# A transformer block in float32 on one core: the copies of the values and the context's keys change their places in the self-attention's slots

## Chip, core and metric

The kernel runs on one core of a Trainium2 chip. The metric is the time of one execution on the device in microseconds (us). TensorE (PE) does matrix products, VectorE (DVE) row maxima and 32x32 transposes, ScalarE (ACT) exponentials and copies out of PSUM, GpSimd (POOL) elementwise work in SBUF, and SyncE (SP) issues nearly all DMAs, in the order in which its queue holds them.

## The reference

Two sequences `x` of 1024 rows by 256, and two contexts of 154 rows by 192, all in float32:

```
h = layernorm(x, ln1);  x = attention(h, h, sa_wq, sa_wk, sa_wv, sa_wo, sa_bo) + x
h = layernorm(x, ln2);  x = attention(h, context, ca_wq, ca_wk, ca_wv, ca_wo, ca_bo) + x
h = layernorm(x, ln3);  a, gate = split(h @ ff_w1 + ff_b1)
x = (a * gelu(gate)) @ ff_w2 + ff_b2 + x
```

Attention has 16 heads of 64 columns, with an ordinary softmax over the keys.

## The kernel before

**Units and slots.** A unit is one sequence and one pair of heads: 2 x 8 = 16 units, 0 to 15. The self-attention of a unit takes eight slots, so there are 128 slots p, with unit p // 8 and place n = p % 8 in it (SH = 4 is half a unit). The order on every engine is written out by hand: the main loop over p (line 1364 on) records one slot after the other, and each engine works off its own list. A slot is counted here on PE, from the first score product (L568) of p to the first of p + 1.

A slot p does this. PE computes the scores of 64 query rows, in two halves (`scores`, L568, two PSUM tiles; a tile is used again in the next slot, once its exponentials are taken). DVE takes their negated maxima (L577), ACT the exponentials and their sums (L585). Each row's keys lie in two halves on two groups of partitions, so the halves' maxima and sums must be exchanged: `exchange` (L595) issues four small DMAs on SP into the tile `st`, once both exponentials are there. In the next slot POOL takes the difference of the maxima (`differences`, L603 and L604, "dd"), ACT its exponential (L610, "ee"), POOL the denominator (L612, L614), and a slot later DVE its reciprocal (L683, "rd"), POOL weighs the exponentials with it (L691), and DVE transposes them (L718).

**Beside the scores** PE has one piece of other work in every slot: in n = 3, 4, 7 and 0 the product of the weights with the values (`self_values`, L624, "po"), in the other four what the list `work` holds: the queries (L395) and keys (L395) of the next unit, values (L427) of the next pair of units, or, in one slot per unit from unit 2 on, a round of the output projection (`out_rounds`, L532, "pr"). In a round the second half waits for a small copy `seen` (L541) on ACT, which stands between the exponentials of the same slot. A layer norm of other rows has its transposes (L307) in n = 5 of some units.

**Values.** `value_pieces` projects the values of units u and u + 1 in two pieces; the second is done in n = 2 of the even unit u, and ACT copies it to SBUF at the start of n = 3 (`store` in `project_self_values`, L437). The product needs each value also on the other 64 partitions: `half_moves` gives two DMAs a unit (L449, L450; 256 KB each). Those of unit u are issued at once in `store`, so on SP ahead of the exchange of n = 3; those of u + 1 go on the list `moves`, of which `load_ahead` issues one in n = 4 and one in n = 5, behind the exchange of that slot. The values of a unit are first read in its n = 7.

**Unit 0 is apart.** Its own queries, its values and those of unit 1 are projected in its slots 0 to 2 (values: two banks `mm_tile`), the queries and keys of unit 1 in slots 3 and 4. Beside them, from the list `side`, come turning the contexts (slot 0), the context's keys of pair 0 (slot 1), of pairs 1 and 2 (slot 2; `context_keys`, L881, 2 products a pair), and turning the rows of gains and shifts (`turn_rows`, L218, slot 3). Slot 5 has the keys of pairs 3 and 4, slot 6 those of pair 5. `context_ends` (L913), the last rows of the context's values for all pairs, is in slot 10, with a `sum_tile`, its weights `ca_wv_ends` (two DMAs of 384 KB, `load_ends`, L898) being issued in slot 4. The key weights of pairs 3 to 5 (`load_keys(3, 3)`, L123, 288 KB) replace those of pairs 0 to 2 in one buffer and are issued in slot 3.

**Weights.** `load_ahead(p)` runs behind the exchange of slot p. In units other than 0 it loads the query weights (L142) of unit u + 2 in n = 2 and its key weights (L142) in n = 6; in unit 0 these are n = 5 and 6. There is one buffer for key weights; they are used in n = 2 or 5 of unit u + 1. `later` holds writes of `ends` to DRAM (L922), popped in n = 2, 4 and 6; `to_dram` lists six slots in which keys go to DRAM (L844).

## Time and profile before

| | us |
|---|---|
| median of 3 runs | 1072.24 |
| the runs | 1070.6, 1072.24, 1075.17 |
| the profiled execution | 1069.05 |
| its span, first to last instruction | 1067.3 |
| scores of slot 0 begin | 17.62 |
| slot 17 (n = 1 of unit 2) begins | 111.25 |
| slot 120 (n = 0 of unit 15) begins | 654.89 |

In the rows of a timeline the first number is the start in us from the span's start, the second the length, then engine, line, operation, what is written and read, and the count of instructions merged into the row. A bracket at the end is idle time of that engine just before the row, and what ended it. Rows of SPq are issues of DMAs: their length is the issue, not the transfer.

### The profile page before, as it was taken

What the parts mean: (1) busy time and instruction counts of PE and PEld (TensorE: products, weight loads), DVE (VectorE), ACT (ScalarE), POOL (GpSimd) and SP (SyncE); (2) the same over time, 40 slices, a digit from 0 to 9 for tenths busy, and PEclk for the clock granted to TensorE, in tenths of its full rate; (3) what the DMA queues carried; (4) which work ended last, traced back from release to release, by engine and by line L of the source; (5) the groups of instructions that cost most, each with busy time, mean ns of one, the idle gap of its engine ahead of it and who ended that gap; (6) DMA issues with size and microseconds to landing.
All of it is one profiled execution on the core that took longest, in us unless ns stands there. A gap on an engine that the chain in (4) does not pass through costs nothing.

```text
span 1067.3 us, 51311 instructions
## 1 busy us (share of the span) xinstructions
PE 1051.0 (98%) x21700; PEld 731.4 (69%) x21700; DVE 882.2 (83%) x1321; ACT 658.6 (62%) x2147; POOL 767.1 (72%) x1604
## 2 busy tenths in 40 slices
PE   8999999999999999999999999999999999999998
PEld 6435755566566668775556686666777667789998
DVE  5689899999989999999999989978776777775654
ACT  5666667667776766766777767666556655243221
POOL 2577677778777787777777777768666677598783
PEclk9999999999999999999999999999999999999999
DMA  4231221121021121121111112135422221000000
GB/s 106 73 83 50 70 63 41 32 47 44 14 64 35 25 54 44 30 50 44 30 41 47 34 35 63 36 77 134 124 59 83 68 59 41 1 7 15 21 11 30
DMA packets 96887, 52.87 MB, mean 50 GB/s; under 512 B 30410, under 2 KB 95442, under 8 KB 96658
## 3 DMA queue, kind: packets, MB, share of 16 engines
q1 hardware_dynamic: 95330, 48.93, 18.6%
q8 instruction: 171, 2.80, 1.1%
q10 hardware_dynamic: 1328, 0.66, 0.2%
q14 instruction: 58, 0.48, 0.1%
HBM read 36.23 MB, written 4.39 MB: 38 GB/s over the span
## 4 chain that ended last, share of the span: by engine, by line
PE 84%; DVE 5%; POOL 3%; ACT 2%; SPq 2%; DMA 2%; issue 2%; DVEq 0%; POOLq 0%; ACTq 0%
PE po L624 18%; PE s L568 18%; PE py_ca L508 5%; PE pv_sa L427 5%; PE pf L1267 4%; PE pq_sa L395 4%; PE pr L532 4%; PE pk_sa L395 4%; PE poc L1042 4%; PE pb L1147 4%; PE pq_ca L395 4%; PE sc L977 3%; PE pa L1147 2%; PE pc L1147 2%; SPq L595 2%
## 5 line engine op out<-in xcount | busy, mean ns | idle before, releaser
L691 POOL TENSOR_SCALAR p<-p,rd,ee 128x512 f32<-128x512 f32 x508 | 385.1, 768 | 78.5 <-DVE rd L683 74.8
L585 ACT ACTIVATE p<-s,st 128x512 f32<-128x512 f32 x512 | 345.3, 685 | 142.7 <-DVE st L577 118.2
L577 DVE TENSOR_REDUCE st<-s 128x2 f32<-128x1024 f32 x256 | 308.5, 1206 | 52.8 <-PE s L568 16.5
L718 DVE STREAM_TRANSPOSE pT<-p 128x1024 f32<-128x1024 f32 x256 | 303.9, 1220 | 2.8 <-POOL p L691 2.8
L568 PE MATMUL s<-k_sa,q_sa 64*32 64x512 f32 x4096 | 256.9, 590 | 3.0 <-ACT p L585 2.4
L624 PE MATMUL po<-pT,v_sa 64*32 64x256 f32 x6144 | 181.0, 376 | 1.9 <-ACT p L995 1.5
L624 PEld LDWEIGHTS po<-pT,v_sa 64*32 64x32 f32 x6144 | 137.3, 106 | 51.4 <-issue 15.0
L568 PEld LDWEIGHTS s<-k_sa,q_sa 64*32 64x32 f32 x4096 | 99.2, 106 | 83.3 <-issue 46.3
L995 ACT ACTIVATE p<-sc,neg 128x154 f32<-128x154 f32 x256 | 96.9, 405 | 72.4 <-DVE rden L1003 70.4
L1006 POOL TENSOR_SCALAR p<-p,rden 128x154 f32<-128x154 f32 x256 | 96.8, 398 | 52.9 <-DVE rden L1003 51.9
L585 ACT ACTIVATION_READ_ACCUMULATOR p<-s,st 128x1 f32 x512 | 103.2, 201 | 0.0
L982 DVE TENSOR_REDUCE neg<-sc 128x6 f32<-128x924 f32 (+1 forms) x48 | 48.1, 1003 | 20.2 <-PE sc L977 20.0
L610 ACT ACTIVATE ee<-dd 128x8 f32<-128x8 f32 x128 | 26.7, 209 | 57.1 <-POOL dd L604 56.1
L508 PE MATMUL py_ca<-ca_wo,o_ca 128*128 128x256 f32 x256 | 61.1, 385 | 0.0
L624 PE MATMUL po<-pT,third_v 64*32 64x256 f32 x2048 | 60.2, 376 | 0.5 <-issue 0.5
L427 PE MATMUL pv_sa<-sa_wv,home 64*32 64x256 f32 x2048 | 59.4, 376 | 0.0
L624 PEld LDWEIGHTS po<-pT,third_v 64*32 64x32 f32 x2048 | 50.5, 106 | 12.8 <-issue 6.1
L395 PE MATMUL pq_ca<-home,ca_wq 64*128 64x512 f32 (+1 forms) x352 | 57.8, 589 | 0.0
L395 PE MATMUL pq_sa<-home,sa_wq 64*32 64x512 f32 (+1 forms) x976 | 57.8, 586 | 0.0
L427 PEld LDWEIGHTS pv_sa<-sa_wv,home 64*32 64x32 f32 x2048 | 46.4, 106 | 15.7 <-issue 5.4
L995 ACT ACTIVATION_READ_ACCUMULATOR p<-sc,neg 128x1 f32 x256 | 56.5, 221 | 0.0
L612 POOL TENSOR_TENSOR zz<-ee,st 128x8 f32<-128x8 f32 x128 | 25.9, 202 | 42.6 <-ACT ee L610 42.6
(142 smaller groups left out, 1604.1 us busy)
## 6 DMA issues: line engine op xcount, KB each, us to landing
st<-st SPq DMA_DIRECT2D x510, 1.0 KB, 2.1
v_sa<-v_sa SPq DMA_DIRECT2D x24, 256.0 KB, 3.8
v_ca<-vd SPq DMA_DIRECT2D x32, 160.0 KB, 3.5
sa_wq<-in_L_xattn_sa_wq_dram SPq DMA_DIRECT2D x32, 128.0 KB, 3.1
sa_wk<-in_L_xattn_sa_wk_dram SPq DMA_DIRECT2D x32, 128.0 KB, 3.2
sa_wv<-in_L_xattn_sa_wv_dram SPq DMA_DIRECT2D x32, 128.0 KB, 3.1
ca_wq<-in_L_xattn_ca_wq_dram SPq DMA_DIRECT2D x32, 128.0 KB, 4.6
wf<-in_L_xattn_ff_w_dram SPq DMA_DIRECT2D x12, 256.0 KB
```

The costliest lines, as they stand in the source:

```text
L395: nc.tensor.matmul(pq[r][f:f + m, at:at + n], lhsT=wt[own, c, f:f + m], rhs=h[own, c, t0:t0 + n], start=(c == 0), stop=(c == NH - 1), tile ...
L427: nc.tensor.matmul(pv[r][f:f + KB, i * VC:(i + 1) * VC], lhsT=h[own, c, t0:t0 + KB], rhs=wt[own, c, :], start=(c == 0), stop=(c == NH - 1) ...
L508: nc.tensor.matmul(py[:, e * D:(e + 1) * D], lhsT=o[:, i, (t + e) * P:(t + e + 1) * P], rhs=wo[kind, b, g][:, i, :], start=(i == 0), stop= ...
L568: nc.tensor.matmul(sc[a4 * KB:(a4 + 1) * KB, j, :], lhsT=q[r, c:c + KB], rhs=k[r, h * HB:(h + 1) * HB], start=True, stop=True, tile_positi ...
L577: nc.vector.tensor_reduce(st[:, 0, 0, i, :], sc, AX.X, ALU.max, negate=True)
L585: nc.scalar.activation(pr[:, j, :], sc[:, j, :], AF.Exp, bias=st[:, 0, 0, i, j:j + 1], accum_out=st[:, 0, 1, i, j:j + 1],)
L624: nc.tensor.matmul(po[a2][d:d + KB, :QH // 2], lhsT=v[r, t, e, d:d + KB], rhs=pT[r, d // DH * NK + n, :], start=(t == 0 and e == 0), stop= ...
L691: nc.gpsimd.tensor_scalar(pr[:, j, :], pr[:, j, :], v["rd"][:, c:c + 1], v["ee"][:, 0, c:c + 1], op0=ALU.mult, op1=ALU.mult,)
L718: nc.vector.transpose(halves[h][:, :, c:c + KB], slot[p]["members"][i].rearrange("p j (n k) -> p (j n) k", k=KB))
L995: nc.scalar.activation(pr_[:, j, i, :T], sc[:, j, i * T:(i + 1) * T], AF.Exp, bias=neg[:, j, i:i + 1], accum_out=den[:, j, i:i + 1],)
L1006: nc.gpsimd.tensor_scalar(pr_[:, j, i, :T], pr_[:, j, i, :T], rden[:, j, i:i + 1], 1.0, op0=ALU.mult, op1=ALU.mult,)
L1147: nc.tensor.matmul(into[:, :BT], lhsT=lhs, rhs=wh[pair][i], start=first, stop=True, skip_group_check=True)
```

## The change

All of it concerns the self-attention.

1. `store` of the values issues no move itself; all four go on `moves`, and `load_ahead` issues one in each of n = 3, 4, 5 and 6 of an even unit, behind that slot's exchange.
2. The context's keys of pairs 0 to 2 leave slots 1 and 2. The keys are now done three at a time (`three_keys`): pairs 0 to 2 in slot 5, pairs 3 to 5 in slot 10. `load_keys(3, 3)` follows the first three, in slot 5. `turn_rows` so comes in slot 1.
3. `context_ends` goes from slot 10 to slot 6, with an `mm_tile`. `load_ends` stays in slot 4. The writes of `ends` so begin four slots earlier.
4. The second value piece of unit 0 takes `sum_tile` banks.
5. The key weights are loaded in n = 7 instead of n = 6, in every unit. The query weights stay.

```diff
@@ store() of project_self_values
             if i0 + 2 == GT:
-                for move in half_moves(v[0]):
-                    move()
-                moves.extend(half_moves(v[1]))
+                for own in v:
+                    moves.extend(half_moves(own))
@@ value_pieces
-    def value_pieces(u, bank):
+    def value_pieces(u, banks):
...
-                [bank(f"pv_sa{u}_{i0}_{r}") for r in range(2)], wsl["sa", pr, "v"], hT["sa", b], i0)
+                [banks[i0 // n](f"pv_sa{u}_{i0}_{r}") for r in range(2)], wsl["sa", pr, "v"], hT["sa", b], i0)
@@ self_beside
             if ui == 1:
-                nxt.insert(1, costing(2, context_ends))
+                nxt.insert(1, costing(2, lambda: three_keys(3)))
             if ui % 2:
-                ahead_values.extend(value_pieces(ui + 1, sum_tile))
+                ahead_values.extend(value_pieces(ui + 1, (sum_tile, sum_tile)))
@@ load_ahead
-            if n != (2 if what == "q" and ui else 2 * SH - 2 - (what == "q")):
+            if n != (2 * SH - 1 if what == "k" else 2 if ui else SH + 1):
...
-        if moves and ui % 2 == 0 and n in (SH, SH + 1):
+        if moves and ui % 2 == 0 and n in range(SH - 1, 2 * SH - 1):
             moves.pop(0)()
...
-        if p == 3:
-            load_keys(3, 3)
@@ new
+    def three_keys(first):
+        return together(*(
+            lambda pr=pr, bank=bank: context_keys(pr, bank)
+            for pr, bank in enumerate((sum_tile, sum_tile, mm_tile), first)))
@@ context_ends
-        pe = sum_tile("pe")
+        pe = mm_tile("pe")
@@ before the main loop
-        side.append((True, (), lambda: context_keys(0, sum_tile)))
-        side.append((True, (), lambda: together(*(
-            lambda pr=pr: context_keys(pr, sum_tile) for pr in (1, 2)))))
         side.append((True, (), turn_rows))
...
-        work.extend(value_pieces(0, mm_tile))
+        work.extend(value_pieces(0, (mm_tile, sum_tile)))
@@ main loop over p
                 if p == SH + 1:
-                    for pr in (3, 4):
-                        run(lambda: context_keys(pr, mm_tile))
+                    run(lambda: three_keys(0))
+                    load_keys(3, 3)
                 elif p == SH + 2:
-                    run(lambda: context_keys(5, mm_tile))
+                    run(context_ends)
```

## The prediction

> **What bounds the kernel now.** First the page's span and a table of busy time by stage (after the span: length, PE busy, PEld, DVE, ACT, POOL, then PE's granted clock, DMA share, GB/s).

> ```profile
> span 1067.3 us, 51311 instructions
> 0.00:150.00 150.00, 141.29 (x3180) 87.41 (x3188) 118.64 (x158) 95.49 (x281) 91.91 (x198) 1.00 0.30 76
> 150.00:700.00 550.00, 548.82 (x14976) 357.81 (x14968) 513.28 (x611) 385.05 (x1166) 417.20 (x864) 1.00 0.17 41
> 700.00:1067.30 367.30, 360.88 (x3568) 286.19 (x3552) 250.26 (x554) 178.06 (x701) 257.99 (x544) 1.00 0.20 52
> ```

> PE is the bound. From 150 to 700 us it is idle 1.2 us of 550, in the first 150 us 8.7 us; nothing after 700 us is touched by the change. DVE is next, 513 of 550. A busy PE need not be at its best pace, so I read the timeline of PE: the time from the first score product of a slot to that of the next.

> ```profile
> 84.32 1.93 PE L568 MATMUL s<-k_sa,q_sa 64*32 64x512 f32 x32
> ...
> 89.49 1.93 PE L568 MATMUL s<-k_sa,q_sa 64*32 64x512 f32 x32
> ```

> That is 5.17 us, the pace of nearly every slot after slot 11: about 1.75 for scores, 3.45 beside them. The work on PE is the same before and after, so a gain can only be stretched slots made short. I find three places.

> **1. Unit 0 and what is moved in it** (slots 0 to 11). PE again; slots 2, 3 and 10 begin with the L568 rows at 28.72, 36.41 and 74.66, slot 12 with that at 84.32 above; the row at 65.18 is the second half of slot 8's scores.

> ```profile
> 28.72 1.95 PE L568 MATMUL s<-k_sa,q_sa 64*32 64x512 f32 x32
> ...
> 34.05 2.42 PE L881 MATMUL pk<-ctxT,ca_wk 96*128 96x320 f32 x8
> 36.41 1.95 PE L568 MATMUL s<-k_sa,q_sa 64*32 64x512 f32 x32
> ...
> 41.72 0.24 PE L218 MATMUL p_rows<-ident,rows 28*128 28x28 f32 x1
> ...
> 51.00 2.39 PE L881 MATMUL pk<-ctxT,ca_wk 96*128 96x320 f32 x8 [1.78 <-DMA ca_wk<-in_L_xattn_ca_wk_dram]
> ...
> 65.18 1.09 PE L568 MATMUL s<-k_sa,q_sa 64*32 64x512 f32 x16 [0.61 <-ACT p L585]
> ...
> 74.66 1.93 PE L568 MATMUL s<-k_sa,q_sa 64*32 64x512 f32 x32
> 76.52 1.92 PE L913 MATMUL pe<-ca_wv_ends,ctxT 96*32 96x512 f32 x16
> ```

> Slot 2 is 7.69 long, because two pairs of keys (2.42, so 1.2 a pair) follow the value piece. Slot 1 loses one pair (1.2) and gains the rows (0.24), slot 2 loses 2.42, slot 3 the rows. The sum is 3.6 us, and slot 5 begins so much earlier; `sum_tile` for the second value piece costs at most the few tenths that ACT's copy of the rows ends after the scores.

> In slot 5 PE was ready for its keys at 51.00 - 1.78 = 49.22 and waited for weights. Now it is ready at 45.6 and the weights of pairs 0 to 2 have long been there: three pairs, 3.6, to 49.2. Scores of slot 6 to 50.9; then `context_ends`, which needs the weights that SP issues at the end of slot 4:

> ```profile
> 46.77 0.54 SPq L123 DMA_DIRECT2D ca_wk<-in_L_xattn_ca_wk_dram  x1
> 47.49 2.90 SPq L595 DMA_DIRECT2D st<-st  x4
> ...
> 52.49 1.64 SPq L898 DMA_DIRECT2D ca_wv_ends<-in_L_xattn_ca_wv_dram  x2
> 54.29 2.47 SPq L595 DMA_DIRECT2D st<-st  x4
> ```
> ```profile
> 60.98 0.20 POOL L603 TENSOR_TENSOR dd<-st 128x8 f32<-128x8 f32 x1 [2.73 <-DMA st<-st]
> ```
> ```profile
> 62.35 0.18 DVE L683 RECIPROCAL rd<-den 128x4 f32<-128x4 f32 x1 [1.97 <-POOL den L614]
> ```

> The 768 KB of `ca_wv_ends` were issued from 52.49. The trace does not show when they land, since slot 10 needed them 24 us later. Bounds: the 288 KB of `ca_wk`, issued at 46.77, were used at 51.00, so at least 4.2 us; the exchange of slot 5, issued behind them, had landed at 60.98, so at most 8.5. I take 6.5, near the middle, as both rows are transfers on that same loaded queue. On SP everything of slot 4 comes 3.6 earlier, and another 0.7 earlier because `load_keys` no longer stands before that slot's exchange (2.90 long instead of the usual 2.4): 4.3. So the weights are issued at 48.2 and land at 54.7 (52.4 to 56.7), and **PE waits 3.8 us (1.5 to 5.8) in slot 6: a new wait**. Behind it in PE's queue are the scores of slot 7, at 54.7 + 1.9 = 56.6, and the first values.

> [...] In this trace PE's clock is 1.00 in all three stretches. [...]

> The chain of slot 5's exchange is 4.3 earlier too: dd at 56.7, rd at 58.05, before the second maxima of slot 7 (about 59). PE then goes on: scores of slot 7 to 58.35, values to 61.8, scores of slot 8 to 63.6, where before they end at 65.18 + 1.09 = 66.3. That is 2.7 us gained. Slot 10 gets three pairs of keys for `context_ends`: slots 10 and 11 took 84.32 - 74.66 = 9.66, and will take 5.25 + 5.17 = 10.4, losing 0.8. **Sum of the first place: -1.9 us** (from -4.9 with no wait at slot 6 but DVE's pace, to 0). `load_keys` now stands before the exchange of slot 6 and may hold it 1 us; its "dd" is queued behind POOL's weighing until about 61, which hides that.

> **2. The moves.** Slot 35 is n = 3 of unit 4. SP, then POOL:

> ```profile
> 210.95 0.62 SPq L449 DMA_DIRECT2D v_sa<-v_sa  x1
> 211.62 0.63 SPq L450 DMA_DIRECT2D v_sa<-v_sa  x1
> 212.41 7.71 SPq L595 DMA_DIRECT2D st<-st  x8
> ```
> ```profile
> 217.95 0.20 POOL L603 TENSOR_TENSOR dd<-st 128x8 f32<-128x8 f32 x1 [1.67 <-DMA st<-st]
> ```

> The two moves push the exchange back by 1.3 us of issue and then by their data; POOL waits 1.67. PE does not feel this at once, having two score tiles, but DVE and ACT are now late, and in n = 6 the second half of a projection round waits for ACT:

> ```profile
> 137.06 2.30 PE L568 MATMUL s<-k_sa,q_sa 64*32 64x512 f32 x32
> ...
> 141.58 1.96 PE L532 MATMUL pr<-sa_wo,o_sa 64*32 64x256 f32 x64 [0.49 <-ACT seen L541]
> 143.33 1.93 PE L568 MATMUL s<-k_sa,q_sa 64*32 64x512 f32 x32
> ...
> 474.56 2.09 PE L568 MATMUL s<-k_sa,q_sa 64*32 64x512 f32 x32
> 480.79 1.93 PE L568 MATMUL s<-k_sa,q_sa 64*32 64x512 f32 x32
> ```

> Slot 22 takes 6.27, slot 86 6.23, 1.1 each above 5.17; the third of this kind, slot 70, is 0.5 over: 2.6 in all. And in units 4 and 6 slots n = 4 and 5 are stretched by 2.1 in all, with PE waiting for nothing that the profile names (slot 36: 6.01 us):

> ```profile
> 211.23 1.92 PE L568 MATMUL s<-k_sa,q_sa 64*32 64x512 f32 x32
> ...
> 217.24 0.66 PE L568 MATMUL s<-k_sa,q_sa 64*32 64x512 f32 x7
> ```

> With the moves behind the exchange, the lateness and its 2.6 us go. Of the unnamed 2.1 I take half: they fall while two query loads and both moves are in flight, which are now spread out, but no row names the cause. **Sum: -3.7 us** (0 to -4.7). What the added places n = 5 and 6 cost can be read from a move that already stands behind an exchange, in slot 38 (PE, SP, POOL):

> ```profile
> 223.40 1.95 PE L568 MATMUL s<-k_sa,q_sa 64*32 64x512 f32 x32
> ...
> 228.60 2.06 PE L568 MATMUL s<-k_sa,q_sa 64*32 64x512 f32 x32
> ```
> ```profile
> 225.95 0.65 SPq L450 DMA_DIRECT2D v_sa<-v_sa  x1
> 228.92 2.44 SPq L595 DMA_DIRECT2D st<-st  x4
> ```
> ```profile
> 233.66 0.20 POOL L603 TENSOR_TENSOR dd<-st 128x8 f32<-128x8 f32 x1
> ```

> PE's slot takes 5.20; 3 us pass before the next exchange, and its "dd" has no bracket: it waited for nothing. [...] The last move leaves in n = 6 of the even unit; unit u's two leave in n = 3 and 4 and are read in n = 7, two slots (10 us) after.

> **3. Key weights.** In slot 15 SP issues keeps, key weights and keys to DRAM before the exchange.

> ```profile
> 104.45 1.35 SPq L142 DMA_DIRECT2D sa_wk<-in_L_xattn_sa_wk_dram  x2
> ...
> 106.61 3.38 SPq L595 DMA_DIRECT2D st<-st  x4
> ```
> ```profile
> 99.81 1.93 PE L568 MATMUL s<-k_sa,q_sa 64*32 64x512 f32 x32
> ...
> 111.25 0.79 PE L568 MATMUL s<-k_sa,q_sa 64*32 64x512 f32 x5
> ```

> The exchange is 1.4 late, and slots 15 and 16 take 11.44, 1.1 over 10.34. With the weights a slot later it is on time; I take half, **-0.5** (0 to -1.1), as the stretched rows name no cause. In other units the load has the 2.6 us between exchanges to itself and is used two slots later at the earliest: 0.

> **Sum:** -1.9 - 3.7 - 0.5 = -6.1 us on the profiled execution's 1069.05, that is 1062.9. That execution was 3.2 us under the median of the runs, 1072.24; the forecast for a median is **1066**.

> **The rivals.**
> A. *The wait at slot 6 eats the first place.* The weights land at the late bound, 2.0 us later than taken, or PE comes back at a lower clock: at half, a stretch as long as the wait (3.8 us) does half its work and loses 1.9. Either leaves 1066 + 2 = 1068. For it: 768 KB are moved up by four slots with nothing to cover them. Against: the exchange behind them bounds it, and in slot 7 DVE is not ready much earlier.
> B. *The stretched slots stay*, since PE shows 1.2 us of idle in 550: then they are of another making, and only 1.9 to 2.5 are won, 1070. Against: the bracket at L532 names ACT.
> C. *Slower: a move in flight stretches PE's slot.* If what makes slot 36 0.84 us too long (6.01 - 5.17) strikes every slot with a move beside it, there are now 28 of these (4 in 7 units), and they lose 23.5, 2.1 of it already lost today, against 5 won elsewhere: 1072 + 21.4 - 5 = 1088. It decides from 7.1 / 28 = 0.25 us a slot on. Against: slot 38 above, with a move in flight, is 0.03 over.
> D. *More*: all of the bounds come, -10 or so: 1062.

> **How the numbers follow.** About 0.5% (5.4 us) is what a measurement of this kernel can tell from no change. Forecast 0.62, of which 0.50 beyond 0.5% and 0.12 within; A 0.13 and B 0.13, within; C 0.06, slower; D 0.06, faster. Faster 0.56, same 0.38, slower 0.06. The range takes the forecast, A, B and D, from -11 to about -1, and 1 us at each end because the three runs of before lie 4.6 apart: 1060 to 1072.

> **What would show it.** Right: slots 2 and 5 at 5.2 to 5.3 us; a PE wait of 2 to 6 us at L913 in slot 6; in even units "dd" of n = 3 with no DMA wait, slots 22 and 86 at 5.2 and no bracket at L532; slots 15 and 16 together under 11. Wrong: L913 waits over 6 us or a granted clock under 1.00 near 55 us; new brackets at "dd" in n = 5 to 7; PE waiting for keys' or queries' weights at L395; stretched slots wherever a move flies.

## The result, and the profile after

| kernel | median, us | runs | ratio to before (95% interval) |
|---|---|---|---|
| before | 1072.30 | 6, 1070.60 to 1075.17 | |
| changed | 1067.78 | 6, 1066.32 to 1069.25 | 0.9958 (0.9941 to 0.9975) |
| changed, second series | 1065.78 | 5, 1064.04 to 1067.64 | 0.9953 (0.9940 to 0.9965), beside a before of 1071.04 |

The change makes the kernel faster by 4.5 to 5.3 us. The forecast was 1066, the range 1060 to 1072. The gain of 0.42% is just inside the 0.5% that the chances called "within", where rival A stood.

The two profiled executions alone would mislead: 1069.05 before, 1069.25 after. The first is faster than all six timed runs of before, the second is the longest of the six after. The page's span and the table by stage of the changed kernel:

```profile
span 1067.5 us, 51300 instructions
0.00:150.00 150.00, 142.88 (x3180) 87.32 (x3188) 118.60 (x158) 95.22 (x281) 91.91 (x198) 0.99 0.29 74
150.00:700.00 550.00, 549.97 (x14978) 360.76 (x14964) 513.04 (x611) 384.90 (x1166) 417.03 (x864) 1.00 0.18 41
700.00:1067.50 367.50, 360.95 (x3568) 286.30 (x3552) 249.83 (x554) 178.33 (x701) 258.27 (x544) 1.00 0.20 53
```

PE is busier in the first 150 us (142.88 for 141.29), with no more work to do. The clock column says why: 0.99 where before had 1.00.

**Unit 0.** Line numbers differ a little between the kernels: L567 here is L568 of before, L915 its L913, L594 its L595. PE in the changed kernel: slots 2, 3, 6 and 7 begin with the first four L567 rows, the last row is the scores of slot 8. Then SP: the exchange of slot 4 and the issue of the weights.

```profile
28.20 1.95 PE L567 MATMUL s<-k_sa,q_sa 64*32 64x512 f32 x32
...
33.39 1.99 PE L567 MATMUL s<-k_sa,q_sa 64*32 64x512 f32 x32
...
49.84 1.95 PE L567 MATMUL s<-k_sa,q_sa 64*32 64x512 f32 x32
55.25 3.40 PE L915 MATMUL pe<-ca_wv_ends,ctxT 96*32 96x512 f32 x16 [3.46 <-DMA ca_wv_ends<-in_L_xattn_ca_wv_dram]
58.58 2.10 PE L567 MATMUL s<-k_sa,q_sa 64*32 64x512 f32 x32
...
63.95 1.90 PE L567 MATMUL s<-k_sa,q_sa 64*32 64x512 f32 x32
```
```profile
44.74 3.59 SPq L594 DMA_DIRECT2D st<-st  x4
...
50.42 1.59 SPq L900 DMA_DIRECT2D ca_wv_ends<-in_L_xattn_ca_wv_dram  x2
```

Slot 2 takes 33.39 - 28.20 = 5.19 (7.69 before). Slot 6 takes 58.58 - 49.84 = 8.74 (4.01 before), with the forecast wait at its product: 3.46 us. What was not in the forecast stands in the lengths: the sixteen products behind the wait take 3.40 us, where they took 1.92 before. The table by stage, cut at the moments where the trace's clock changes (same columns), shows PE's clock at half:

```profile
52.15:55.56 3.41, 0.31 (x4) 0.16 (x8) 3.41 (x5) 2.78 (x8) 2.28 (x4) 1.00 1.01 251
55.56:58.97 3.41, 3.41 (x24) 0.56 (x24) 0.23 (x1) 0.48 (x2) 0.94 (x5) 0.50 0.69 162
58.97:62.39 3.42, 3.42 (x104) 1.75 (x96) 2.38 (x4) 1.44 (x4) 1.63 (x3) 1.00 0.37 103
```

**The moves.** SP, POOL and PE, slot 36 and what follows; these answer to the rows of slots 35 and 36 before.

```profile
212.14 3.12 SPq L594 DMA_DIRECT2D st<-st  x4
215.31 0.66 SPq L448 DMA_DIRECT2D v_sa<-v_sa  x1
```
```profile
216.98 0.20 POOL L602 TENSOR_TENSOR dd<-st 128x8 f32<-128x8 f32 x1
```
```profile
211.97 1.92 PE L567 MATMUL s<-k_sa,q_sa 64*32 64x512 f32 x32
...
217.14 1.92 PE L567 MATMUL s<-k_sa,q_sa 64*32 64x512 f32 x32
```

The exchange now leaves ahead of the move, "dd" has no bracket (1.67 before), and slot 36 takes 5.17 (6.01 before; other traces with the old moves have 5.17 to 5.20 there too).

**The key weights.** SP, POOL and PE around slots 16 to 19.

```profile
109.26 1.34 SPq L142 DMA_DIRECT2D sa_wk<-in_L_xattn_sa_wk_dram  x2
110.65 1.76 SPq L843 DMA_DIRECT2D kd<-home  x1
112.57 2.47 SPq L594 DMA_DIRECT2D st<-st  x4
```
```profile
118.13 0.20 POOL L602 TENSOR_TENSOR dd<-st 128x8 f32<-128x8 f32 x1 [1.95 <-DMA st<-st]
```
```profile
121.37 0.64 PE L567 MATMUL s<-k_sa,q_sa 64*32 64x512 f32 x5
...
127.43 0.79 PE L567 MATMUL s<-k_sa,q_sa 64*32 64x512 f32 x4
```

They now stand with a write of keys to DRAM (L843) ahead of the next exchange. Its "dd" waits 1.95 us, and slot 19, from 121.37 to 127.43, takes 6.06 instead of 5.17. This comes and goes: a second trace of the same kernel has no such wait in slot 18 and 5.17 in slot 19.

### The profile page after: what moved, and what is told of

The parts are those of the page before. It is cut to its first block, busy times and chain, and to the rows that moved or that the text cites. A ratio compares the mean times of both kernels' runs of the same rounds, so it can differ in the third digit from the quotient of the medians.

```text
span 1067.5 us, 51300 instructions
## 1 busy us (share of the span) xinstructions
PE 1053.8 (99%) x21700; PEld 734.4 (69%) x21700; DVE 881.5 (83%) x1321; ACT 658.5 (62%) x2147; POOL 767.2 (72%) x1604
## 4 chain that ended last, share of the span: by engine, by line
PE 84%; DVE 4%; POOL 3%; DMA 3%; ACT 2%; issue 2%; SPq 2%; POOLq 0%; DVEq 0%; ACTq 0%
PE po L623 18%; PE s L567 18%; PE py_ca L507 5%; PE pr L531 5%; PE pv_sa L427 5%; PE pf L1269 4%; PE pk_sa L395 4%; PE pq_sa L395 4%; PE poc L1044 4%; PE pb L1149 4%; PE pq_ca L395 4%; PE sc L979 3%; DMA st<-st 3%; PE pa L1149 2%; PE pc L1149 2%; POOL p L690 2%
## 5 line engine op out<-in xcount | busy, mean ns | idle before, releaser
L567 PE MATMUL s<-k_sa,q_sa 64*32 64x512 f32 x4096 | 260.7, 590 | 0.6 <-DVE k_sa L416 0.6
L567 PEld LDWEIGHTS s<-k_sa,q_sa 64*32 64x32 f32 x4096 | 100.5, 107 | 82.2 <-issue 52.3
L395 PE MATMUL pq_sa<-home,sa_wq 64*32 64x512 f32 (+1 forms) x976 | 58.9, 586 | 0.0
L395 PE MATMUL pq_ca<-home,ca_wq 64*128 64x512 f32 (+1 forms) x352 | 57.8, 589 | 0.0
L395 PE MATMUL pk_sa<-home,sa_wk 64*32 64x512 f32 x960 | 57.1, 589 | 0.0
```

Of the source, the lines that this page charges most:

```text
L395: nc.tensor.matmul(pq[r][f:f + m, at:at + n], lhsT=wt[own, c, f:f + m], rhs=h[own, c, t0:t0 + n], start=(c == 0), stop=(c == NH - 1), tile ...
L567: nc.tensor.matmul(sc[a4 * KB:(a4 + 1) * KB, j, :], lhsT=q[r, c:c + KB], rhs=k[r, h * HB:(h + 1) * HB], start=True, stop=True, tile_positi ...
```

## Thirteen traces side by side

Every experiment left a trace. This table has the start of slots 0, 12 and 120 in each (first score product), and from these the time of slots 0 to 11 (unit 0 and half of unit 1) and of slots 12 to 119 (all the other units that the moves touch). The last column is the time that the trace shows at clock 0.50 behind a wait of PE in unit 0.

| kernel | slot 0 | slot 12 | slot 120 | 0 to 11 | 12 to 119 | at 0.50 |
|---|---|---|---|---|---|---|
| before | 17.62 | 84.32 | 654.89 | 66.70 | 570.57 | 0 |
| context edits alone | 17.67 | 85.27 | 657.97 | 67.60 | 572.70 | 6.83 |
| key weights alone | 17.63 | 84.66 | 656.06 | 67.03 | 571.40 | 0 |
| early weights, old moves | 17.69 | 80.24 | 653.01 | 62.55 | 572.77 | 0 |
| changed | 17.79 | 84.72 | 655.12 | 66.93 | 570.40 | 3.41 |
| changed, second trace | 17.59 | 84.54 | 651.71 | 66.95 | 567.17 | 6.83 |
| moves alone | 17.65 | 87.67 | 655.13 | 70.02 | 567.46 | 6.83 |
| moves alone, weights first | 17.62 | 85.25 | 652.48 | 67.63 | 567.23 | 0 |
| weights ahead in slot 4 | 17.64 | 81.73 | 650.26 | 64.09 | 568.53 | 0 |
| early weights | 17.72 | 80.21 | 648.29 | 62.49 | 568.08 | 0 |
| early weights, key weights back | 17.61 | 81.24 | 648.31 | 63.63 | 567.07 | 0 |
| early weights, moves in pairs | 17.63 | 81.97 | 648.82 | 64.34 | 566.85 | 0 |
| early weights, other bank | 17.75 | 79.89 | 649.70 | 62.14 | 569.81 | 0 |

Two things are seen at once. With the old moves (first four rows) slots 12 to 119 take 571.9 on average, with the new ones (nine rows) 568.1: 3.8 us less. And one kernel differs from itself by 3.2 us there (570.40 and 567.17), so no single trace carries an argument about 3 us.

## The experiments

### The three edits, each by itself

**The moves alone.** The kernel before with

```diff
-                for move in half_moves(v[0]):
-                    move()
-                moves.extend(half_moves(v[1]))
+                for own in v:
+                    moves.extend(half_moves(own))
...
-        if moves and ui % 2 == 0 and n in (SH, SH + 1):
+        if moves and ui % 2 == 0 and n in range(SH - 1, 2 * SH - 1):
```

> The kernel before with the values' moves put behind the exchange in n = 3 to 6, and nothing else. Theory of the prediction: the late exchange of n = 3 is what stretches n = 6 of even units, so -3.7 us against before (0.9966), slots 22, 70 and 86 at 5.2 and no ACT bracket at the second half of their projection round. Rival (the stretched slots are of another making and come and go from one execution to the next): within 1 us of before, with stretched slots of the same total elsewhere. Rival C (a move in flight stretches the slot it lies beside): slower.

1068.47 us (12 runs), 0.9972 (0.9962 to 0.9983): -3.0 us. Slots 22, 70 and 86 take 5.58, 5.17 and 5.38, and no trace with the new moves has more than a bracket of 0.16 at the second half of the round. Rival C is out. The price is in unit 0, where the first move now stands ahead of the weights of context pairs 3 to 5; PE in slot 5:

```profile
52.78 4.60 PE L880 MATMUL pk<-ctxT,ca_wk 96*128 96x320 f32 x8 [3.42 <-DMA ca_wk<-in_L_xattn_ca_wk_dram]
57.31 2.61 PE L567 MATMUL s<-k_sa,q_sa 64*32 64x512 f32 x32
```

The wait is 3.42 (1.78 before), and the eight products behind it take 4.60 instead of 2.39.

**The context edits alone.** The changed kernel with the moves and the key weights of before, that is with the lines of the diff above and of the diff below put back.

> The kernel before with the context's keys three at a time, the last value rows' product in slot 6 and the bank of the second value piece, moves and key weights as before. By the traces of before and after, slots 0 to 11 are the same length in both (66.7 and 66.9 us): what slots 1 to 3 win (3.4 us) is lost to the wait for the weights in slot 6 (3.46 us). So 0 within 1 us. The prediction on record gave -1.9 (0.9982). PE's wait at the product of slot 6 should be there, 3 to 4 us.

1072.57 us (12 runs), 1.0009 (0.9996 to 1.0023). The expected nothing, then, and no sign of -1.9. The trace has the wait (2.83 us) and 6.83 us of half clock behind it; PE's column and the clock:

```profile
51.41:54.82 3.41, 0.92 (x8) 0.16 (x8) 3.41 (x5) 2.79 (x8) 2.27 (x3) 1.00 0.84 223
54.82:58.23 3.41, 3.22 (x28) 0.65 (x32) 0.26 (x1) 0.79 (x2) 1.59 (x5) 0.50 0.78 194
58.23:61.65 3.42, 3.42 (x48) 1.08 (x40) 2.15 (x3) 1.23 (x3) 1.09 (x3) 0.50 0.34 93
```

The 12 executions differ in the clock that the whole execution was granted: two had 1.000 and took 1068.5 on average, four had 0.998 (3.41 us at half out of 1070 give that) and took 1072.4, six had 0.997 (6.83 us) and took 1073.8. Two executions are few, and those may have waited less as well. Nor is before free of this, though its one trace shows none of it: of its 51 executions beside the experiments, 16 had a clock of 0.998 or less.

**The key weights alone.** The kernel before with

```diff
-            if n != (2 if what == "q" and ui else 2 * SH - 2 - (what == "q")):
+            if n != (2 * SH - 1 if what == "k" else 2 if ui else SH + 1):
```

> The kernel before with only the key weights a slot later, in n = 7. The prediction on record: -0.5 us. What the trace of after says: slots 15 and 16 get 0.6 shorter together, but in n = 0 of units 2 and 3 the weights now stand on SP with a write of keys to DRAM ahead of the next exchange, whose differences then wait 2.0 us, and a slot 5 to 8 us later is stretched by 0.5 to 0.9: so +0.5 to +1 us (1.0005 to 1.001), with waits of 2 us at the differences of slots 17 or 18 and 25.

1071.06 us (12 runs), 0.9998 (0.9986 to 1.0010): nothing. The late "dd" is there in slot 18 (1.65 us, a wait that this trace puts down to no DMA), slot 19 takes 5.83, and slot 25 has none. The forecast gain is not there to be had: slots 15 and 16, 11.44 long in the trace of before, take 10.34 in the traces of the moves alone and of the context edits alone, where the key weights stand as before. That stretch came and went with the execution. And the late exchange is not new with the edit, only a slot later. With the key weights in n = 6, "dd" waits 1.97 to 2.59 us in slot 17 in four of five traces, and slot 18 behind it takes 5.34 to 5.82. With them in n = 7, it waits 1.56 to 1.95 us in slot 18 in five of eight, and slot 19 takes 5.73 to 6.06.

### The wait in slot 6

**Weights in slot 2.** The changed kernel with one line moved:

```diff
-        if p == SH:
+        if p == 2:
             load_ends()
```

> The changed kernel with the weights of the last value rows issued in slot 2 instead of slot 4, and nothing else. Theory: the wait of 3.46 us in slot 6 is the whole cost of the edit in unit 0, so it goes and the time is 3 to 3.5 us under the changed kernel's, about 7.5 to 8 under before (0.993). Rival (the wait only hides one behind it, as DVE and the exchanges of unit 0 bound the slots): under 1 us better than the changed kernel, 0.995, with a new bracket in slots 7 or 8.

1061.80 us (4 runs), 0.9910 (0.9896 to 0.9924), the fastest kernel of this study: 6.0 us under the changed kernel's first series and 4.0 under its second, by the medians more than the wait of 3.46 alone. Slots 0 to 11 take 62.49 instead of 66.9. PE from slot 6:

```profile
51.49 1.92 PE L915 MATMUL pe<-ca_wv_ends,ctxT 96*32 96x512 f32 x16
53.63 1.09 PE L567 MATMUL s<-k_sa,q_sa 64*32 64x512 f32 x16 [0.21 <-ACT p L584]
54.97 1.09 PE L567 MATMUL s<-k_sa,q_sa 64*32 64x512 f32 x16 [0.25 <-ACT p L584]
```

No wait, the products back at 1.92, and what is late next is ACT, for 0.46 us. The rival (something hidden behind the wait) is out.

**Weights ahead of the other loads in slot 4.** A dose in between: the same lines ahead of the value weights and the move of slot 4, instead of behind them.

```diff
         ui, n = divmod(p, 2 * SH)
+        if p == SH:
+            load_ends()
         for what in "qk":
...
-        if p == SH:
-            load_ends()
```

> The changed kernel with the weights of the last value rows still issued in slot 4, but ahead of that slot's value weights and move instead of behind them. That brings them 2.05 us sooner (issue at 50.42 less 48.37), so the wait in slot 6 falls from 3.46 to about 1.4 us. Theory: the wait of 3.46 us also halved PE's clock for 3.41 us behind it, at a price of 1.7 us, and the shorter wait does not; so 2.05 + 1.7 = 3.7 us under the changed kernel, and the clock stays at 1.00. Rival (the clock goes down after any wait of PE in that place): 2.0 us under, clock 0.50 for 3.4 us. Second rival (DVE bounds the next slots): under 1 us.

1062.36 us (6 runs), 0.9919 (0.9903 to 0.9936): 5.4 us under the changed kernel's first series by the medians, 4.2 by the ratios, and 3.4 and 3.6 under its second. Expected were 3.7, and 2.0 without the clock. PE, and the clock of the stretch with the wait:

```profile
52.47 1.06 PE L915 MATMUL pe<-ca_wv_ends,ctxT 96*32 96x512 f32 x8 [0.90 <-DMA ca_wv_ends<-in_L_xattn_ca_wv_dram]
54.06 1.07 PE L915 MATMUL pe<-ca_wv_ends,ctxT 96*32 96x512 f32 x8 [0.53 <-DMA ca_wv_ends<-in_L_xattn_ca_wv_dram]
```
```profile
49.03:52.45 3.42, 2.53 (x35) 0.63 (x33) 3.22 (x5) 2.48 (x9) 2.46 (x7) 1.00 0.91 251
```

The wait is 1.43 in two parts, the products run at full speed (2.13 in all), the clock stays. By the trace, slots 0 to 11 win 2.8 (66.93 to 64.09). The series lie too far apart (1067.78 and 1065.78) to tell 2.8 from 3.7.

**The changed kernel once more**, with no edit.

> The changed kernel once more, for a second trace and more executions. Theory: the wait in slot 6 takes PE's clock to half in most executions, so the trace shows a stretch at 0.50 right behind it of 3.4 us or a multiple, the executions with the longer stretch are the longer ones, and slots 12 to 119 take 568 us as in the other kernels with the new moves (the first trace, with 570.4, was long there by chance). Time 0.995 to 0.997. Rival: slots 12 to 119 take 570.4 again, so the changed kernel has stretched slots of its own there.

1065.78 us, slots 12 to 119 in 567.17: the first trace's 570.40 was chance. Ten of the eleven executions of the changed kernel, in the two series, had a granted clock under 1.000. That those with the longer half clock are the longer ones is not seen in this series: 1065.78 at 0.996, 1065.79 on average at 0.998 (three), 1065.92 at 1.000. The second trace has the other length of the half clock; first PE, then the table by stage:

```profile
54.05 3.64 PE L915 MATMUL pe<-ca_wv_ends,ctxT 96*32 96x512 f32 x16 [3.56 <-DMA ca_wv_ends<-in_L_xattn_ca_wv_dram]
57.62 2.88 PE L567 MATMUL s<-k_sa,q_sa 64*32 64x512 f32 x32
```
```profile
49.34:52.75 3.41, 1.15 (x24) 0.15 (x8) 3.21 (x5) 2.87 (x9) 2.83 (x7) 1.00 0.99 243
52.75:56.16 3.41, 2.11 (x12) 0.55 (x16) 1.74 (x2) 1.09 (x4) 0.72 (x1) 0.50 0.62 155
56.16:59.58 3.42, 3.42 (x32) 0.66 (x32) 0.00 (x0) 0.79 (x2) 1.59 (x5) 0.50 0.75 193
```

**The moves alone, context weights first.** The moves alone, and

```diff
         ui, n = divmod(p, 2 * SH)
+        if p == 3:
+            load_keys(3, 3)
         for what in "qk":
...
-        if p == 3:
-            load_keys(3, 3)
```

> The kernel before with the moves alone put behind the exchanges, as in the run of the moves alone, and with the key weights of context pairs 3 to 5 issued ahead of the move in slot 3 instead of behind it. In the run of the moves alone that move pushed these weights back, PE waited 3.42 us for them in slot 5 (1.78 before) and had half its clock for 6.83 us. Theory: this cost about 3 us of what the moves won, so this kernel is 3 us under the run of the moves alone, 5.5 to 6.5 under before (0.9945), slot 5 at 6 us or less and the clock at 1.00. Rival: the moves are worth 3 us and no more: 0.997 again.

1067.49 us (8 runs), 0.9965 (0.9950 to 0.9981). The wait in slot 5 and the half clock are gone from the trace, slots 0 to 11 take 67.63 instead of 70.02, but the time is only 1.0 us better, inside the intervals. My theory that this cost 3 us is not borne out; the trace of the moves alone had one of the worse starts (the twelve executions went from 1065.94, at a clock of 1.000, to 1070.93, at 0.997).

### What the moves are worth, and why

**Early weights with the old moves.** The kernel with the weights in slot 2, with the diff of the moves alone put back.

> The kernel with the weights of the last value rows issued in slot 2, with the moves put back as before (two at once ahead of the exchange of n = 3, two behind those of n = 4 and 5). This prices the moves where no wait in unit 0 disturbs them. Theory of the prediction: 2.8 us by the traces (slots 19 to 119 take 534.8 on average in the three traces with the old moves, 532.0 in the three with the new), so 1064.5 to 1066 (0.994 of before). Rival (moves are worth 6 us outside unit 0): 1068, 0.997. Rival (nothing): 1062, 0.991.

1066.36 us (6 runs), 0.9957 (0.9940 to 0.9973): 4.6 us above the same kernel with the new moves. Unit 8 shows the mechanism. With the new moves, SP, then POOL, then PE from the start of slot 70:

```profile
374.28 2.75 SPq L594 DMA_DIRECT2D st<-st  x4
377.07 0.66 SPq L448 DMA_DIRECT2D v_sa<-v_sa  x1
```
```profile
378.99 0.20 POOL L602 TENSOR_TENSOR dd<-st 128x8 f32<-128x8 f32 x1
```
```profile
384.39 1.96 PE L567 MATMUL s<-k_sa,q_sa 64*32 64x512 f32 x32
386.10 3.70 PE L531 MATMUL pr<-sa_wo,o_sa 64*32 64x256 f32 x128
389.56 1.96 PE L567 MATMUL s<-k_sa,q_sa 64*32 64x512 f32 x32
```

With the old ones, the same three engines:

```profile
375.36 0.62 SPq L449 DMA_DIRECT2D v_sa<-v_sa  x1
376.02 0.64 SPq L450 DMA_DIRECT2D v_sa<-v_sa  x1
376.82 7.10 SPq L595 DMA_DIRECT2D st<-st  x8
```
```profile
383.35 0.20 POOL L603 TENSOR_TENSOR dd<-st 128x8 f32<-128x8 f32 x1 [2.28 <-DMA st<-st]
```
```profile
386.45 2.27 PE L568 MATMUL s<-k_sa,q_sa 64*32 64x512 f32 x32
388.43 4.53 PE L532 MATMUL pr<-sa_wo,o_sa 64*32 64x256 f32 x128
392.66 2.01 PE L568 MATMUL s<-k_sa,q_sa 64*32 64x512 f32 x32
```

The late exchange costs POOL 2.28 us, and three slots after the moves the projection round takes slot 70 to 6.21 (5.17 with the new moves). The thirteen traces agree on this place. Where that "dd" waits 1.66 to 1.70 us (four traces, two of them with the new moves), slot 70 takes 5.56 to 5.68; at 1.83 it takes 5.87, at 2.28 6.21, and with no wait there 5.17 to 5.35. So the new order makes the lateness rare, not impossible.

**Early weights, moves in pairs.** Behind the exchange, but two in n = 3 and two in n = 4:

```diff
-        if moves and ui % 2 == 0 and n in range(SH - 1, 2 * SH - 1):
-            moves.pop(0)()
+        if moves and ui % 2 == 0 and n in (SH - 1, SH):
+            moves.pop(0)()
+            moves.pop(0)()
```

> The kernel with the weights of the last value rows in slot 2; the moves all behind the exchange, but two at once in n = 3 and two at once in n = 4, instead of one in each of n = 3 to 6. Theory (the order is what counts: an exchange that is not behind a move on SP is on time): as with one a slot, 1061 to 1063, 0.991, slots 22, 70 and 86 at 5.2 to 5.6. Rival (the spreading counts: 512 KB in flight hold the next exchange): 1064 to 1066, waits of 1 us or more at the differences of n = 4 or 5 of even units, and slots 22, 70 and 86 at 6.

1063.01 us (5 runs), 0.9924 (0.9911 to 0.9938). Slots 22, 70 and 86 take 5.65, 5.17 and 5.28, slots 12 to 119 take 566.85. In units 2, 6 and 8 "dd" waits 0.06 us at most in n = 4 and 5, in the other even units from unit 4 on 0.68 at most. It is the order, then; spreading the moves is worth 1.2 us at most by the medians, and the intervals overlap.

**Early weights, key weights back in n = 6.** The kernel with the weights in slot 2, with the diff of the key weights alone put back.

> The same kernel with the weights of the last value rows in slot 2, with the key weights put back into n = 6. The prediction gave the key weights -0.5 us; the run of the key weights alone gave 0 within 1.3. Theory: no difference, within 0.7 us of the kernel with both (0.991). Rival: 1 us or more to either side, since in n = 0 of units 2 and 3 they meet the writes of keys to DRAM.

1062.54 us (6 runs), 0.9916 (0.9898 to 0.9935): nothing to tell apart, as expected.

**Early weights, other bank.**

```diff
-            for pr, bank in enumerate((sum_tile, sum_tile, mm_tile), first)))
+            for pr, bank in enumerate((mm_tile, sum_tile, sum_tile), first)))
```

> The kernel with the weights of the last value rows in slot 2, and the three pairs of keys taking the mm_tile first instead of last. Theory: in slot 5 the first pair waits for a sum_tile until ACT has copied the keys of unit 1 out of it (ACT's copy ends at 46.1, PE's keys begin at 46.4, 0.86 us after the scores could be done), so slot 5 falls from 6.04 to 5.2 and the time by 0 to 0.8 us. Rival (something else stretches these scores): slot 5 stays at 6.0.

1061.93 us (5 runs), 0.9920 (0.9907 to 0.9932). Slot 5 takes 5.81. Without this edit it takes 6.04 in four traces and 5.47 to 5.88 in others, so the bank is not shown to be what stretches it; neither theory holds, and the cause stays open.

## Why the prediction was right, and where it was not

The time lies in the range, but of the three terms only the moves came about as forecast.

**First place: -1.9 forecast, nothing measured; rival A happened.** Slots 0 to 11 take 66.93 and 66.95 in the two traces, 66.70 before. The step that failed is "PE then goes on: scores of slot 7 to 58.35", which lets PE leave the wait at full clock. In the first trace, sixteen products took 3.40 instead of 1.92 and the scores behind them 2.10 instead of 1.93: 1.65 us, and the forecast's 2.7 us of gain at slot 8 became 0.6 (its scores end 63.95 + 1.90 - 0.17 for the later start = 65.68, not 66.27). The other 0.4 us is the weights, ready at 55.25 - 0.17 = 55.08 and not at 54.7. With wait and half clock both gone (weights in slot 2), slots 0 to 11 take 62.49, 4.2 under before; the bound for that was -4.9.

Rival A had this mechanism, with 1.9 us as its price and 1068 as its time, and the prediction's sign of being wrong came too: a clock under 1.00 near 55 us. Rival A was given 0.13, beside a trace of before that showed 1.00 throughout; but in that trace PE's longest wait in slots 1 to 11 was 1.78. A trace with a short wait says nothing of a long one. That PE might come back at half clock was supposed in the prediction, and no row of before shows it; the runs do: the waits were 3.46 and 3.56 us, and behind each the clock was at 0.50, for 3.41 and 6.83 us.

The size of the wait was right (3.8 forecast, 3.46 and 3.56 measured), but by two errors that met. The weights left SP at 50.42, not 48.2: slot 4's exchange came only 2.75 earlier (44.74 for 47.49), not 4.3, and took 3.59 on SP. And they landed 55.25 - 50.42 = 4.83 us after their issue, not 6.5; the lower bound (4.2) was the better row. Slot 5, forecast at 5.25, took 6.04 and 5.47.

**Moves: -3.7 forecast; -3.0 (1.8 to 4.1) alone, -4.6 with the early weights, -3.8 over all traces.** Right in mechanism, and in size within the intervals. The named part did not go wholly: slot 22 takes 5.49 to 5.93 in the new traces (6.27 to 6.72 in the old), slot 86 5.27 to 5.65 (5.36 to 6.72 in the old); the three slots 22, 70 and 86 together lose 2.2 us on average, of the forecast 2.6. Of the unnamed 2.1, half of which was taken, only the part in slot 52 belongs to the old moves: it takes 5.77 to 6.06 in the four old traces and 5.17 to 5.31 in the nine new ones, 0.8 less on average. Slot 53 kept its 6.2 to 6.4 in all thirteen, and slot 36 was stretched only in the one trace of before. That half of 2.1 came close to this 0.8 is luck.

**Key weights: -0.5 forecast, 0 measured.** The step that failed is "in other units the load has the 2.6 us between exchanges to itself": a write of keys to DRAM is there in units 2 and 3, and in the traces the late exchange came a slot later instead of going. And the 11.44 us that were to shrink were 10.34 in two other traces with the key weights in the same place; what stretched them in the trace of before stays open.

**The sum.** The parts measured alone give -3.0 + 1.0 - 0.2 = -2.2, the whole -4.5 (-2.7 to -6.3). The moves alone met their own late weights in unit 0, which the context edits take out of the way; that this is the whole of the difference is not shown, and each of the parts is known to 1 us only. That the whole came near the forecast of -6.1, with two of the three terms at nothing, is in part luck.

## What to carry to other kernels

Where an edit leaves a wait on TensorE as long as those here (2.83 to 3.56 us), count the half clock behind it too, here 1.65 us beside a wait of 3.46; issuing the load two slots sooner was worth about as much as the whole change (4.0 to 6.0 us beside 4.5 to 5.3). Small exchanges that an engine waits for go ahead of bulk copies on a queue, whether these follow singly or in pairs (here 1061.80 and 1063.01 us, with two of the four copies ahead 1066.36). Before a stretched slot of one trace is put into a sum, look for it in a second trace of the same program.

## What was not expected of the hardware

```profile
47.55:50.97 3.42, 1.67 (x32) 0.48 (x16) 2.34 (x4) 1.89 (x6) 1.78 (x4) 1.00 0.49 133
```

PE was busy 1.67 of 3.42 (49%), and the next stretch had full clock. It was busy 0.31, 0.92 and 1.15 (9%, 27%, 34%) in the stretches shown above at 1.00 ahead of those at 0.50. The trace of the moves alone has 26%:

```profile
48.49:51.90 3.41, 0.88 (x19) 0.00 (x0) 2.83 (x4) 1.88 (x6) 2.04 (x3) 1.00 0.73 156
```

So a wait of 2.83 was enough. The end of the kernel with the weights in slot 2, where PE has run out of work, adds a point:

```profile
1056.03:1059.44 3.41, 1.39 (x13) 1.19 (x11) 1.31 (x3) 0.00 (x0) 0.00 (x0) 1.00 0.23 77
```

PE was busy 41%, idle for the last 2.03 us of the stretch, and the clock was at 0.50 from 1059.44 on. In the trace of before and the first of the changed kernel, from where the clock is on record (6.59 and 7.77 us) to the end, and in the stretches printed here of the others, no stretch at full clock with 49% or more was followed by half clock, and every one with 41% or less was, so the edge lies between these two. Whether the share or the length of the idle time inside the stretch counts, these traces do not tell: both put them in the same order at the edge (1.75 us idle before, 2.03 here). Back came the clock after a half-clock stretch that PE filled (3.41 of 3.41, or 3.42 of 3.42); after those with 2.11, 2.54 (of the moves alone) and 3.22 busy it stayed at half for one more. The grid lies differently from one execution to another (a boundary at 55.56 in one trace of the changed kernel, at 52.75 in the other), which fits that one kernel comes with half clocks of 3.41 and of 6.83 us.
